# The order of square transfers and the tiles of a weight expansion in a fused attention, MLP and adapter kernel

## The chip, the cores and the metric

The kernel runs on one core of one Trainium2 chip. The core has TensorE (PE; its weight loads are listed as PEld), VectorE (DVE), ScalarE (ACT), GpSimd (POOL) and SyncE (SP). SP, ACT and POOL issue transfers, each on a queue of its own (q1, q10 and q0 in the profile); 16 DMA engines carry them. The metric is the device time of one execution in microseconds. The kernel before took 1170.44 us (median of 3 runs, 1168.72 to 1171.33).

## What is computed

Four sequences of 512 tokens by 512 features, float32. For each sequence b:

```
q, k, v  = x @ Wq, x @ Wk, x @ Wv
attn_out = softmax(q k^T / sqrt(512)) @ v @ Wp + bp
cms      = gelu(attn_out @ cW1 + cb1) @ cW2 + cb2 + one_hot(code_b)     # 512 -> 2048 -> 512
modifier = gelu([attn_out, cms] @ mW1 + mb1) @ mW2 + mb2                # 1024 -> 2048 -> 512
y        = clip(x + cms + modifier, 0, 1)
h        = y + gelu(y @ W_down[s] + b_down[s]) @ W_up[s] + b_up[s]      # s = stream_b, one of 3 adapters
out      = layernorm(h) * ln_w[s] + ln_b[s]
```

## The kernel before

**Products by seven.** Large products are done by a two-by-two block scheme with seven products in place of eight (Strassen's, in Winograd's form), mostly at two levels. Each product needs sums of weight blocks and sums of input blocks. PE does the products, DVE and ACT put them together, and the sums of weight blocks are formed once: `weight_sums` (L236, operations at L238, L241, L242, L243) makes the four sums of a block on POOL. This is called expansion here. Expanded weights go to DRAM (`c1_inner`, `c1_outer`, `c2_kept`, `m1_kept`, `m2_kept`, in the profile `c_inner`, `c_outer`, `c_kept`, `m_kept`) and SP fetches them when the layers run.

**The stages.** The sequences are taken in two pairs. First Wq is folded with Wk, and Wv with Wp (`folded`). Then attention for pair 0 and pair 1 (to about 237 us), then for pair 0 the first cms layer (`c1_layer`, to about 330 us), the second (`second_layer` with cW2, from about 330 us), the two modifier layers, and the same for pair 1 with the adapters of pair 0 between. The expansion of cW1, cW2 and mW1 (`expansion`, L449) runs on POOL beside the attention and the first cms layer, handed out in steps by `steps(expanding, n)`; that of mW2 comes later.

**The tiles.** SBUF is full, so tiles have many uses. `wide` holds slots 0 and 1; slots 2 to 7 are tiles of their own (all shown as `slot` in the profile), 1 MB each; `part` has 1 MB, `first` 0.5 MB. The expansion reads raw weights in slots 4 and 5 and writes slot 1, slot 3, `part` and `first`. Slot 6 holds Wv and slot 7 Wp until they are folded; then they take x of sequences 3 and 2.

**Squares.** `load_squares` (L153) loads x of a sequence of the second pair as 32-by-32 squares, four transfers per sequence, for DVE to transpose (L534). The 128-byte rows make 2048 packets per transfer. The call is at L995, first for sequence 2 (slot 7), then for sequence 3 (slot 6), on SP's queue.

**Order.** A scheduler arranges each engine's instructions from the program's order and its own estimates; what is passed to `tc.keep_in_program_order` keeps its place. Each engine then runs its list in order, and waits by semaphores for what its operands need: a write into a tile waits for transfers that still read it.

**One unit of the expansion.** `expand_c1` (L268) makes one of two units of cW1: sums of one block in the upper half of slot 1 (transfer L275), sums of the outer level into the lower half of slot 1, `part` and `first` (transfers L286 and L287), and the sums of those in slot 1 (transfer L291). Both units use slot 1. `expand` (L378) makes one unit of cW2 or mW1, of which there are two and four, with three tiles that are called one, two and three, here `part`, slot 3 and slot 1:

```
tt(s1, a21, a22, ALU.add)             # lower half of one        (L390)
tt(s2, s1, a11, ALU.subtract)         # lower half of two
tt(s3, a11, a21, ALU.subtract)        # lower half of three
yield from plain((2, a12, one), (1, a11, three), (4, a22, two))   # upper halves, each kept (L393)
tt(block(last), a12, s2, ALU.subtract)                            # into first
then()                                                            # raw weights of the next unit (L376)
yield from full((5, one), (7, three), (6, two))                   # upper halves, whole tile kept
yield from fourth(block(last), one)                               # upper half of one, L407 and L408
```

So tile one is written and kept last, by L408, and the sums for L408 wait until the whole of tile one has been kept for product 5.

**Where the tiles are next used.** In the second cms layer `wide` takes differences of the first layer's outputs: `differences(1, LOW)` writes slot 0 and `differences(1, HIGH)` slot 1 (both L1383, DVE). Behind it on DVE come the sums for the next inner operands (L248) and the additions that empty PE's banks (L1067). `part` takes products of the second layer from the fourth outer product on.

Of the kernel before, what the change touches and what calls it, by code (L numbers as in the profile page):

```python
# [18 lines left out]
def kernel(  # L19
# [38 lines left out]
    nc = tc.nc  # L58
# [36 lines left out]
    slot = [wide[:, 4 * i : 4 * i + 4, :].rearrange("p c n -> p (c n)") for i in range(2)]  # L95
    slot += [const.tile([P, 2048], F32, name=f"slot{i}") for i in range(2, 8)]
    wslot = [const.tile([P, 2048], F32, name=f"wslot{i}") for i in range(4)]
    part = const.tile([P, 4, 512], F32, name="part")
    first = const.tile([P, 2, 512], F32, name="first")
# [41 lines left out]
    def flat(t):  # L141
        return t.rearrange("p c n -> p (c n)")
# [10 lines left out]
    def load_squares(src, dst, eng):  # L153

        squares = src.rearrange("(t r) (d a c) -> a r d t c", r=32, a=4, c=32)
        for a in range(4):
            eng.dma_start(
                out=dst[32 * a : 32 * a + 32].rearrange("p (d t c) -> p d t c", d=4, c=32),
                in_=squares[a],
            )  # L160
        return dst.rearrange("p (d t c) -> p d t c", d=4, c=32)

    def load_blocks(src, dst, eng):
# [10 lines left out]
    def load_c1(u, eng):  # L174
        for m in range(2):
            raw = slot[4 + m].rearrange("p (c h n) -> p c h n", c=4, h=2)
            for h in range(2):
                at = h * HH + m * 512 + u * 256
                eng.dma_start(
                    out=raw[:, :, h, :],  # L180
                    in_=cW1[:, at : at + 256].rearrange("(c p) n -> p c n", p=P),
                )

    wp = rows_of(slot[7])
    for a in range(4):
        nc.sync.dma_start(
            out=wp[32 * a : 32 * a + 32],
            in_=Wp[P * a : P * a + P].rearrange("(c p) n -> p c n", p=32),
# [10 lines left out]
    for v, n in zip(bias_src, counts):  # L199
        nc.gpsimd.dma_start(  # L200
            out=bias_rows[at : at + n, :], in_=v.rearrange("(c p) -> c p", p=P)
# [34 lines left out]
    def weight_sums(a11, a12, a21, a22, s1, s2, s3, s4, eng=None, pinned=False):  # L236
        op = (eng or nc.gpsimd).tensor_tensor
        i = op(s1, a21, a22, ALU.add)  # L238
        if pinned:
            tc.keep_in_program_order(i)  # L240
        op(s2, s1, a11, ALU.subtract)  # L241
        op(s3, a11, a21, ALU.subtract)  # L242
        return op(s4, a12, s2, ALU.subtract)  # L243

    def token_sums(b11, b12, b21, b22, t1, t2, t3, t4, eng=None, pinned=False):
# [16 lines left out]
    c1_inner = {  # L262
        (p, u): spill.tile([P, n], F32, name=f"c1_inner_{p}_{u}")
        for p, n in ((1, 1024), (5, 2048), (2, 1024))
        for u in range(2)
    }

    def expand_c1(u, then):  # L268
        raw = [t.rearrange("p (c h n) -> p c h n", c=4, h=2) for t in slot[4:6]]
        to = slot[1][:, 1024:].rearrange("p (k n) -> p k n", k=4)  # L270
        inner_sums = [to[:, k] for k in range(4)]
        weight_sums(
            raw[0][:, 0, 0, :], raw[0][:, 1, 0, :], raw[1][:, 0, 0, :], raw[1][:, 1, 0, :], *inner_sums
        )
        nc.gpsimd.dma_start(out=c1_inner[1, u], in_=slot[1][:, 1024:])  # L275
        yield
        spaces = (slot[1][:, :1024], flat(part)[:, :1024], flat(part)[:, 1024:], flat(first))
        sums = [t.rearrange("p (m c n) -> p m c n", m=2, c=2) for t in spaces]
        for m in range(2):
            weight_sums(  # L280
                raw[m][:, 0:2, 0, :], raw[m][:, 2:4, 0, :], raw[m][:, 0:2, 1, :], raw[m][:, 2:4, 1, :],
                *(t[:, m] for t in sums),
            )
        then()
        outer = c1_outer[u].rearrange("p k m c n -> p (k m c n)")
        nc.gpsimd.dma_start(out=outer[:, :2048], in_=flat(part))  # L286
        nc.gpsimd.dma_start(out=outer[:, 2048:], in_=flat(first))  # L287
        yield
        s1 = sums[0]
        weight_sums(s1[:, 0, 0, :], s1[:, 0, 1, :], s1[:, 1, 0, :], s1[:, 1, 1, :], *inner_sums)  # L290
        nc.gpsimd.dma_start(out=c1_inner[5, u], in_=slot[1])  # L291
        yield

    def c1_plain(p, g, m):
# [69 lines left out]
    def load_raw(src, is_first, u, raw):  # L364
        for h in range(2):
            dst = raw[h].rearrange("p (c n) -> p c n", c=4)
            for i in range(2):
                if is_first:
                    at = i * HH + u * 256
                    rows = src[h * V : (h + 1) * V, at : at + 256]  # L370
                    to = dst[:, :, i * 256 : (i + 1) * 256]
                else:
                    at = h * HH + i * HH // 2 + u * 256
                    rows = src[at : at + 256, :]
                    to = dst[:, 2 * i : 2 * i + 2, :]
                nc.gpsimd.dma_start(out=to, in_=rows.rearrange("(c p) n -> p c n", p=P))  # L376
# [56 lines left out]
    def expand_all(units, raw, pairs, last, end=None):  # L433
        if last is None:
            load_raw(*units[0][:2], units[0][3], raw)
        for n, unit in enumerate(units):

            def then():
                if n + 1 < len(units):
                    load_raw(*units[n + 1][:2], units[n + 1][3], raw)  # L440
                elif end is not None:
                    end()

            yield from expand(unit, raw, pairs, last, then)

    m1_units = [(mW1, True, m1_kept, u) for u in range(4)]
    m2_units = [(mW2, False, m2_kept, u) for u in range(2)]

    def expansion():  # L449

        c2_units = [(cW2, False, c2_kept, u) for u in range(2)]
        yield from expand_c1(0, lambda: load_c1(1, nc.gpsimd))
        yield from expand_c1(1, lambda: load_raw(cW2, False, 0, slot[4:6]))

        constants()
        yield from expand_all(
            c2_units + m1_units, slot[4:6], (flat(part), slot[3], slot[1]), flat(first)
        )

    def late_expansion():  # L460
# [39 lines left out]
    def steps(gen, n):  # L500
        with tc.issue_after(behind.pop().ins) if behind else nullcontext():
            for _ in range(n):
                next(gen, None)

    expanding = expansion()


# [59 lines left out]
    def constants():  # L567

        nc.gpsimd.tensor_copy(pos, pos_i)


        nc.gpsimd.tensor_copy(code, code_i)
        for b in range(B):
            nc.gpsimd.tensor_scalar(target[:, b, :], pos, code[:, b : b + 1], None, ALU.is_equal)
            nc.gpsimd.tensor_add(target[:, b, :], target[:, b, :], cb2_c)


        nc.gpsimd.tensor_copy(ex, str_i)
        nc.gpsimd.tensor_scalar(wrap, ex, 0.0, float(E), ALU.is_lt, ALU.mult)
        nc.gpsimd.tensor_add(ex, ex, wrap)  # L580
        nc.gpsimd.tensor_scalar(ex, ex, 0.0, float(E - 1), ALU.max, ALU.min)
        nc.gpsimd.tensor_copy(idx_e, ex)
        nc.gpsimd.tensor_scalar(ex_v, ex, float(V), None, ALU.mult)
        nc.gpsimd.tensor_scalar(ex_bn, ex, float(BN), None, ALU.mult)
        for b in range(B):
            nc.gpsimd.tensor_scalar(idx_d[:, b, :], pos, ex_v[:, b : b + 1], None, ALU.add)
            nc.gpsimd.tensor_scalar(idx_u[:, b, :], pos[:, :NB], ex_bn[:, b : b + 1], None, ALU.add)
# [379 lines left out]
    for pair in range(B // 2):  # L967
# [3 lines left out]
        u = big[4 - 2 * pair : 6 - 2 * pair]  # L971
# [18 lines left out]
        if pair == 0:  # L990

            lhs_vp = folded(
                left_operand(wv_t, s_v), rhs_wp, w_vp, s_v, order=(1, 5, 6, 2, 7, 3, 4)
            )
            x_blocks = [load_squares(x[b], flat(x_places[b]), nc.sync) for b in range(2, B)]  # L995
# [719 lines left out]
    for pair in range(B // 2):  # L1715
# [43 lines left out]
        for _ in between:  # L1759
# [4 lines left out]
        spaces = [  # L1764
            (h[3][:, 2 * s : 2 * s + 2], h[1][:, 4 * s : 4 * s + 4], (h[2][:, :4], h[3][:, 4:])[s])
            for s in range(2)
        ]
# [92 lines left out]
```

## Time and profile before

| | |
|---|---|
| median of 3 runs | 1170.44 us |
| the profiled execution's own time | 1169.09 us |
| its span, first to last instruction | 1167.2 us |
| mean granted clock of PE | 0.997 |
| DVE, ACT, POOL busy | 77%, 25%, 51% of the span |
| moved by DMA | 258.88 MB, mean 222 GB/s |
| packets under 512 bytes | 24532 of 101442 |

A line of a timeline has the start in the span, the length (of a merged run of like instructions), engine, line, operation, what is written and read, the shape, a count, and in brackets the idle time of the engine before it and what ended that. Buffer numbers are left out, so all tiles of one name look alike. A line of the table by stretches has the stretch, its length, the busy time of PE, PEld, DVE, ACT and POOL with the number of instructions, the granted clock, the DMA engines' busy share and GB/s. A line on a queue has packets, MB and the share of the 16 engines' time; one on an issue has what is written and read, the queue, the count, the size and the time to landing. A mean over the span says little here, since the stages have different limits: what counts is where PE idles and who ended that wait.

### The profile page before, as it was taken

How to read it: one execution, taken by the hardware profiler on the slowest of the kernel's cores; microseconds unless marked ns; L12 is line 12 of the kernel's file. 1: busy time of each engine (PE TensorE's matmuls, PEld its weight loads, DVE VectorE, ACT ScalarE, POOL GpSimd, SP SyncE). 2: the span in 40 equal slices, each digit the busy share in tenths (PEclk: the TensorE clock that was granted, in tenths of full speed). 3: DMA queues.
4: the chain of work that ended last, by engine and by line, in shares of the span. 5: the costliest groups of instructions: out<-in, count | busy, mean ns of one | idle time of the engine just before them, and what ended most of it. 6: DMA issues, size and time to landing. Idle time of an engine off the chain costs nothing.

```text
span 1167.2 us, 13674 instructions
## 1 busy us (share of the span) xinstructions
PE 1155.0 (99%) x4941; PEld 923.9 (79%) x4941; DVE 894.2 (77%) x1227; ACT 293.9 (25%) x535; POOL 593.0 (51%) x646
## 2 busy tenths in 40 slices
PE   9999999999989999999999999999999999999997
PEld 8588468566458888888888887778888888888875
DVE  5755855487699967898699956689994588689955
ACT  4234326245520000013310037272000003230014
POOL 5789989789970058895200676971000001265401
PEclk9999999999999999999999999999999999999999
DMA  9892973898875488888847562145745464575701
GB/s 293 240 252 97 350 311 132 343 367 285 305 266 210 164 277 325 283 317 323 259 153 288 180 218 90 64 152 184 286 143 189 155 230 167 180 271 198 249 4 72
DMA packets 101442, 258.88 MB, mean 222 GB/s; under 512 B 24532, under 2 KB 59648, under 8 KB 86144
## 3 DMA queue, kind: packets, MB, share of 16 engines
q1 hardware_dynamic: 78144, 159.27, 38.9%
q0 software_dynamic: 20848, 89.18, 21.6%
q10 hardware_dynamic: 2384, 9.57, 2.0%
q8 instruction: 39, 0.64, 0.2%
q14 instruction: 27, 0.22, 0.1%
HBM read 188.78 MB, written 66.06 MB: 218 GB/s over the span
## 4 chain that ended last, share of the span: by engine, by line
PE 72%; POOL 16%; DMA 7%; issue 3%; DVE 1%; DVEq 0%; POOLq 0%
PE i L1363 29%; PE i L1463 28%; PE sum L1205 7%; DMA m_kept<-part 4%; PE down_ps L1570 2%; PE up_ps L1589 2%; POOL part L241 1%; POOL slot L376 1%; POOL part L238 1%; DMA c_outer<-part 1%; POOL part L242 1%; POOL wide L238 1%; PE sum L746 1%; DMA c_kept<-wide 1%; POOL part L243 1%
## 5 line engine op out<-in xcount | busy, mean ns | idle before, releaser
L1363 PE MATMUL i<-slot,wslot 128*128 128x256 f32 x1184 | 261.0, 379 | 0.0
L1363 PEld LDWEIGHTS i<-slot,wslot 128*128 128x128 f32 x1184 | 224.9, 190 | 31.0 <-DMA wslot<-in_L_cond_mW 0.4
L1463 PE MATMUL i<-slot,wslot 128*128 128x256 f32 x896 | 204.6, 381 | 4.5 <-DVE cms L1067 4.1
L1463 PEld LDWEIGHTS i<-slot,wslot 128*128 128x128 f32 x896 | 171.2, 191 | 28.9 <-DVE cms L1067 4.5
L1463 PE MATMUL i<-hidden,wslot 128*128 128x256 f32 x576 | 132.2, 379 | 0.0
L1463 PEld LDWEIGHTS i<-hidden,wslot 128*128 128x128 f32 x576 | 109.4, 190 | 15.7 <-issue 1.0
L1074 ACT COPY first<-i 128x512 f32<-128x512 f32 (+1 forms) x42 | 21.6, 514 | 391.3 <-PE i L1363 234.7
L1067 DVE TENSOR_TENSOR part<-i,part 128x512 f32<-128x512 f32 (+1 forms) x156 | 90.8, 591 | 38.1 <-PE i L1363 27.9
L1096 ACT ACTIVATE hidden<-hidden,bias 128x512 f32<-128x512 f32 x128 | 83.9, 716 | 72.1 <-DVE hidden L590 62.0
L1746 POOL DMA_DIRECT2D slot<-xT_kept x4 | 2.9, 729 | 152.9 <-PE i L1363 152.9
L1205 PE MATMUL sum<-mod,wslot 128*128 128x256 f32 x288 | 66.6, 379 | 0.0
L1205 PEld LDWEIGHTS sum<-mod,wslot 128*128 128x128 f32 x288 | 54.7, 190 | 7.4
L248 DVE TENSOR_TENSOR slot<-hidden 128x1024 f32<-128x1024 f32 x46 | 60.6, 1317 | 0.0
L1749 POOL TENSOR_TENSOR cms<-cms,slot 128x512 f32<-128x512 f32 x16 | 23.9, 1516 | 70.3 <-PE i L1363 38.5
L248 DVE TENSOR_TENSOR slot<-hidden,slot 128x1024 f32<-128x1024 f32 x46 | 56.7, 1232 | 0.3
L1295 PE MATMUL c<-slot,wslot 128*128 128x512 f32 x128 | 55.3, 592 | 0.0
L1067 DVE TENSOR_TENSOR part<-i,first 128x512 f32<-128x512 f32 (+1 forms) x50 | 31.4, 632 | 31.1 <-PE i L1363 20.0
L376 POOL DMA_DIRECT2D slot<-in_L_cond_mW x24 | 17.9, 751 | 72.1 <-DVE slot L248 71.1
L746 PE MATMUL sum<-hidden,wslot 128*128 128x256 f32 x232 | 53.2, 379 | 0.0
L590 DVE TENSOR_TENSOR sum<-sum,wslot 128x512 f32<-128x512 f32 x48 | 33.2, 695 | 24.3 <-PE sum L746 19.6
L590 DVE TENSOR_TENSOR hidden<-part,hidden 128x2048 f32<-128x2048 f32 x20 | 48.9, 2446 | 0.5
L1295 PEld LDWEIGHTS c<-slot,wslot 128*128 128x128 f32 x128 | 24.3, 190 | 30.6 <-issue 28.5
(338 smaller groups left out, 2166.1 us busy)
## 6 DMA issues: line engine op xcount, KB each, us to landing
wslot<-m_kept SPq DMA_DIRECT2D x48, 1024.0 KB, 6.5
wslot<-m_kept SPq DMA_DIRECT2D x36, 512.0 KB, 4.9
wslot<-c_kept SPq DMA_DIRECT2D x16, 1024.0 KB, 6.4
slot<-in_L_cond_mW POOLq DMA_DIRECT2D x24, 512.0 KB, 7.7
wslot<-in_L_cond_mW SPq DMA_DIRECT2D x24, 512.0 KB, 6.3
wslot<-in_L_cond_cW SPq DMA_DIRECT2D x40, 256.0 KB, 5.3
slot<-in_L_cond_cW POOLq DMA_DIRECT2D x12, 512.0 KB, 6.9
m_kept<-wide POOLq DMA_DIRECT2D x6, 1024.0 KB, 8.6
```

The lines of the kernel that those rows point to most:

```text
L238: i = op(s1, a21, a22, ALU.add)
L248: i = eng.tensor_tensor(out_, one, two, ALU.subtract)
L376: nc.gpsimd.dma_start(out=to, in_=rows.rearrange("(c p) n -> p c n", p=P))
L590: nc.vector.tensor_tensor(dst, a, b, ALU.add)
L746: nc.tensor.matmul(v[:, j, :], lhsT=lhs[p][:, c, j * P : (j + 1) * P], rhs=rhs[p][:, c, :], start=(first_ and j == 0 and c == 0), stop=(c ...
L1067: nc.vector.tensor_tensor(dst, ps, other, ALU.add)
L1096: nc.scalar.activation(block[:, t, :], block[:, t, :], AF.Gelu, bias=bias_c[:, 8 * half + t : 8 * half + t + 1],)
L1205: nc.tensor.matmul(halves_of(ps)[:, j, :], lhsT=a[g][:, at_[q], j * P : (j + 1) * P], rhs=rhs[q][:, 0, :], start=(first_ and j == 0), stop ...
L1295: nc.tensor.matmul(ps, lhsT=lhs(c, t), rhs=operands[p][:, c, :], start=(c == 0), stop=(c == 1),)
L1363: nc.tensor.matmul(out_ps[:, j, :], lhsT=a[j][q][:, c, :], rhs=now[q][:, c, :], start=(c == 0), stop=(c == 1),)
L1463: nc.tensor.matmul(ps[:, :256], lhsT=a[k // 2][q][:, k % 2, :], rhs=now[q][:, k, :], start=(k == 0), stop=(k == 3),)
L1749: nc.gpsimd.tensor_tensor(cms[s][:, d, :], cms[s][:, d, :], in_rows[3][:, d, :], ALU.add)
```

## The change

Three edits. The eight square transfers are kept in program order, so they go to SP's queue as four for slot 7 and then four for slot 6; before, the scheduler had put three of slot 6 ahead of those for slot 7. The second unit of cW1 forms its sums in slot 3 instead of slot 1. The units of cW2 and mW1 take slot 1, `part`, slot 3 as one, two and three, instead of `part`, slot 3, slot 1.

```diff
@@ load_squares
         for a in range(4):
-            eng.dma_start(
+            i = eng.dma_start(
                 out=dst[32 * a : 32 * a + 32].rearrange("p (d t c) -> p d t c", d=4, c=32),
                 in_=squares[a],
             )
+            tc.keep_in_program_order(i)
@@ expand_c1
-        to = slot[1][:, 1024:].rearrange("p (k n) -> p k n", k=4)
+        place = slot[(1, 3)[u]]
+        to = place[:, 1024:].rearrange("p (k n) -> p k n", k=4)
...
-        nc.gpsimd.dma_start(out=c1_inner[1, u], in_=slot[1][:, 1024:])
+        nc.gpsimd.dma_start(out=c1_inner[1, u], in_=place[:, 1024:])
         yield
-        spaces = (slot[1][:, :1024], flat(part)[:, :1024], flat(part)[:, 1024:], flat(first))
+        spaces = (place[:, :1024], flat(part)[:, :1024], flat(part)[:, 1024:], flat(first))
...
-        nc.gpsimd.dma_start(out=c1_inner[5, u], in_=slot[1])
+        nc.gpsimd.dma_start(out=c1_inner[5, u], in_=place)
@@ expansion
         yield from expand_all(
-            c2_units + m1_units, slot[4:6], (flat(part), slot[3], slot[1]), flat(first)
+            c2_units + m1_units, slot[4:6], (slot[1], flat(part), slot[3]), flat(first)
         )
```

## The prediction

> **What bounds the kernel now.** I read the page first: the busy line says that TensorE (PE) works for 99% of the span, so what a change in the preparation of weights can give or take is only idle time of PE, or its clock.
>
> ```profile
> PE 1155.0 (99%) x4941; PEld 923.9 (79%) x4941; DVE 894.2 (77%) x1227; ACT 293.9 (25%) x535; POOL 593.0 (51%) x646
> ```
>
> Then the busy times by stretch, to find where PE idles. Outside of the first microsecond and the last 28 us there is one place: 325 to 375 us. The second column is PE's busy time, the value after POOL's count is the granted clock.
>
> ```profile
> 325.00:350.00 25.00, 20.70 (x84) 15.50 (x82) 23.60 (x19) 5.24 (x9) 16.76 (x20) 1.00 0.74 271
> 350.00:375.00 25.00, 24.81 (x107) 21.53 (x108) 24.62 (x32) 0.70 (x2) 0.00 (x0) 0.93 0.45 174
> ```
>
> PE's timeline names the wait, and that of DVE shows what DVE did until it freed PE at 350.19.
>
> ```profile
> 344.17 1.96 PE L1463 MATMUL i<-slot,wslot 128*128 128x256 f32 x8 [0.44 <-ACT mod L1074]
> 350.19 5.41 PE L1463 MATMUL i<-slot,wslot 128*128 128x256 f32 x16 [4.06 <-DVE cms L1067]
> ```
>
> ```profile
> 338.65 4.28 DVE L1383 TENSOR_TENSOR wide<-hidden,hidden 128x2048 f32<-128x2048 f32 x1 [1.36 <-DMA m_kept<-wide]
> 342.86 1.21 DVE L248 TENSOR_TENSOR slot<-hidden 128x1024 f32<-128x1024 f32 x1
> 347.51 2.28 DVE L1383 TENSOR_TENSOR hidden<-hidden,hidden 128x2048 f32<-128x2048 f32 x1
> 349.72 0.75 DVE L1067 TENSOR_TENSOR cms<-i,mod 128x256 f32<-128x256 f32 x2
> ```
>
> The second layer begins at 329.8. DVE must write the upper half of `wide`, which is slot 1, and waits for the last transfer of the expansion that reads slot 1; the four L248, one more L1383 and the sums L1067 that empty PE's banks stand behind it in order. So PE's 4.06 us hang on one thing: when the expansion on POOL gives slot 1 back. POOL's timeline shows the expansion's stalls and its last issue:
>
> ```profile
> 54.48 1.27 POOL L242 TENSOR_TENSOR part<-slot 128x512 f32<-128x512 f32 x1 [7.99 <-issue]
> ...
> 62.20 0.72 POOL L238 TENSOR_TENSOR wide<-slot 128x256 f32<-128x256 f32 x1 [4.04 <-DMA c_inner<-wide]
> ...
> 163.63 0.72 POOL L238 TENSOR_TENSOR part<-first 128x256 f32<-128x256 f32 x1 [2.71 <-DMA c_kept<-part]
> ...
> 334.36 0.55 POOL L393 DMA_DIRECT2D m_kept<-wide  x1
> ...
> 341.27 0.55 POOL L408 DMA_DIRECT2D m_kept<-part  x1
> ```
>
> **The change, step by step.** Compared engine by engine, the two programs have the same instructions in the same order on PE, DVE and ACT; POOL and SP differ.
>
> *1. Squares.* Three of the eight square transfers left SP at 42.07 and landed 13.9 us later; now all eight wait for slot 7, so they start at 59.64, where the fourth does now. On SP nothing is queued behind them before the x rows at 128.85, and the first reader is DVE's L534 at 124.15, over 50 us after they can land: no cost there, and if that cover were gone it would be PE's wait for the second pair. POOL's queue gains in 42 to 56 us and loses later. The five that now run at 59.6 to 70.5 moved 10320 packets in 76.4% of 10.9 us, 1.65 us a square, so three are 5.0 us of all 16 DMA engines that move behind 59.64.
>
> *2. Sums in slot 3.* The 7.99 us stall before 54.48 is the first unit's transfer out of `part` (issued 43.27, 11.1 us to landing: 54.4). POOL now has other work first: a slot-3 sum that needs the third raw load, issued 41.79, landing 7.5 us later at 49.3. The stall becomes 49.3 - 46.5 = 2.8 us, 5.2 saved; `part` is written 5.8 us of work after that, at 55.1, when it is free. The 4.04 us wait for slot 1 is gone. Next is the 0.56 us wait for `part` at 86.74, which slot 1 as first tile avoids. A new wait is possible where POOL overwrites `wslot` at 80.70 now; 9.2 us sooner is 71.5, and PE reads it until 71.5: nothing. Slot 3 now has to drain before its L390: issue to landing was 10.1 us for the same megabyte (80.12 to 90.2), so 70.9 + 10.1 = 81.0 against 80.6 wanted: 0.4 lost. Lead of POOL at 90 us: 5.2 + 4.0 + 0.6 - 0.4 = 9.4; if the three squares hold up everything behind 59.64 by their 5.0 us, 4.4.
>
> *3. What is left of the lead.* Here I choose by this row of transfers, 132 to 164 us:
>
> ```profile
> q0 software_dynamic: 1290, 5.73, 45.5%
> q10 hardware_dynamic: 576, 4.19, 31.1%
> q1 hardware_dynamic: 1018, 2.02, 21.6%
> ```
>
> The 16 DMA engines are busy 98% of 32 us: 31.5 us of work, over half of it x rows and kept results that SP and ACT issue when DVE and PE let them, from 128.85 on, and these don't move. POOL's wait at 163.63 is for a transfer in this jam. Issued earlier it only stands longer in the same queue. Of the work, some 1.0 MB of q0 (its 5.73 less the 4.72 up to and with that transfer, 2.6 us) need not come first. Data starts 1.7 us after an issue (a 1 MB transfer alone took 4.2 us, 2.5 of it at 421 GB/s), so the jam starts at 130.5 and that transfer lands between 130.5 + 31.5 - 2.6 = 159.4 and 162.0, against 163.6: a lead of 1.5 to 4.2 us survives, and the rest comes back as a wait of up to 9 us. I take 2.8, the middle. Behind it POOL waits 3.40, 1.41 and 1.38 us at 213 to 227, 1.13 and 1.99 at 254 to 258, 2.59 at 297, all for its own transfers; a lead can shrink to nothing in these or win some 2 us. I leave it at 2.8.
>
> *4. Tiles in another order.* Now the price. The wait at 338.65 was for the transfer of 334.36, slot 1 being the third tile. As first tile, slot 1 is read by the very last transfer (issue 341.27 now, out of `part`). That one took
>
> ```profile
> m_kept<-part POOLq DMA_DIRECT2D x1, 512.0 KB, 9.8
> ```
>
> because SP's loads, issued at 341.17, ran beside it; the same three transfers ended at 127.20 with
>
> ```profile
> c_kept<-part POOLq DMA_DIRECT2D x1, 512.0 KB, 4.6
> ```
>
> Issued 2.8 us sooner, at 338.5, it is ahead of SP's data (341.17 + 1.7 = 342.9), so I take 4.6: landing 343.1. POOL is then done, and DVE's L1383 takes the 2.28 us of the row at 347.51 in place of 4.28: it ends at 345.4 in place of 342.9. DVE is 2.5 us late, PE idles 6.6 us in place of 4.06.
>
> *Sum.* 0 for PE until 346, + 2.5 us there: 1169.09 + 2.5 = 1171.6 us for the profiled execution, which stands 1.35 under the median of the runs; the median becomes 1170.44 + 2.5 = **1172.9 us**. Equal time needs the transfer to land by 340.65, the last issue by 336.05, a lead of 5.2.
>
> The clock: after the 4.06 us idle the profile grants 0.50 at 352 to 354 us, about 3.4 us in all at half speed, 1.7 us lost, and none after the 0.44 us idle. I leave the 1.7 us as it is. The Trainium skill (TensorE: Matmul & The Clock Gate, "What's actually happening") says that the gate looks at free-running windows of 3413 ns, so a later restart can fall into a second slow window. With a restart at 352.7 that would lose some 0.75 us more, 1173.6; no row here shows a second window.
>
> For the squares, the share of the queues at 46 to 48 us is 45.1% for SP's and 43.6% for POOL's. The Trainium skill (DMA: Bandwidth & Descriptors, "Queues, rings and completion order") says that an engine goes round the queues packet by packet, which by that rule would halve POOL's raw loads behind 59.64 and speaks against the change. It would bring the lead at 90 us to the lower 4.4; by the jam behind 132 us the sum stays the same.
>
> **Rivals.**
> *The lead survives (faster).* The place is the wait at 163.6, and it decides from a lead of 5.2 us on. For it: POOL loses 29 us to stalls between 46 and 309 us, the two longest go, and 88 to 104 us is almost free of transfers. Against it: the jam. With all 9.3 us the last issue is at 332.0, landing 336.6, before DVE is free at 337.3: L1383 ends at 339.6, 3.3 us sooner, PE idles 0.7 us, and the 1.7 us of clock come back: -5.0, 1165.4 us.
> *The lead is lost wholly.* The later stretches set the end and the last issue stays at 341.27, beside SP's loads: landing 351.1, L1383 ends at 353.4, 10.4 us late: 1180.8 us. For it: the waits at 213 to 297 are all for queues that SP shares; against it: POOL starts each of them sooner.
> *Gain and price cancel.* A lead of 4.7 to 5.7 us changes nothing: 1170.4 us.
>
> **How the numbers follow.** Forecast 0.50, with its own range 1171.4 (lead 4.2: landing 341.7, +1.0) to 1175.1 (lead 1.5: landing 344.4, +3.8, and 0.9 for SP's loads beside it); lead survives 0.28; lost 0.14; cancel 0.08. About 0.2%, 2.3 us, is what a measurement of this kernel can tell from no change. Slower by more: 0.37 of the forecast's 0.50 and the 0.14, 0.51. Faster by more: a lead over 6 us, where the clock's 1.7 us come too, 0.20. The rest, 0.29, is within. The range leaves out the far thirds of the two outer rivals: 1166.5 to 1179.5.
>
> **What would show it.** Right: POOL has no stalls of 7.99 and 4.04 us and is about 9 us ahead at 75 us; a wait of 6 to 9 us at about 161 on a transfer out of `wide`; last issue at 337 to 340; DVE's L1383 `wide` waits for that last transfer, 4 us or more, and then takes 2.28; PE's idle before L1463 is 5 to 8 us. Wrong, if POOL passes 164 us over 5 us ahead and DVE finds slot 1 free, or if PE idles anywhere new before 330.

## The result, and the profile after

The changed kernel takes 1175.49 us (median of 22 runs, 1170.23 to 1181.56), the kernel before beside it 1169.72 us (median of 22, 1167.46 to 1172.56). The ratio is 1.0049, 95% interval 1.0033 to 1.0065: slower by 0.5%, or 5.8 us. The 22 times are not one spread. They lie in two groups of eleven, 1170.23 to 1174.33 (median 1171.93) and 1176.65 to 1181.56 (median 1179.67), and the median falls between the two. The gap between them is 2.3 us, the widest between neighbours in the list, with 1.8 us the next. The profiled execution took 1173.6 us (span 1171.7) and is of the lower group; it is read first. The changed file's lines are one or two higher: L1383 is now L1385, L1463 L1465, L1067 L1069, L393 L395, L408 L410, L238 L239.

POOL's timeline of the kernel after (start, length, engine, line, operation, tiles, shape, count, idle before and who ended it), with the waits of the expansion and its last issues:

```profile
46.80 0.73 POOL L239 TENSOR_TENSOR slot<-slot 128x256 f32<-128x256 f32 x1 [1.16 <-DMA slot<-in_L_cond_cW]
...
160.82 0.73 POOL L239 TENSOR_TENSOR wide<-first 128x256 f32<-128x256 f32 x1 [13.03 <-DMA c_kept<-wide]
...
207.37 0.72 POOL L239 TENSOR_TENSOR wide<-first 128x256 f32<-128x256 f32 x1 [0.68 <-DMA m_kept<-wide]
...
254.54 0.72 POOL L239 TENSOR_TENSOR wide<-first 128x256 f32<-128x256 f32 x1 [4.26 <-DMA m_kept<-wide]
295.35 0.73 POOL L239 TENSOR_TENSOR wide<-first 128x256 f32<-128x256 f32 x1 [4.76 <-DMA m_kept<-wide]
...
338.84 0.55 POOL L409 DMA_DIRECT2D m_kept<-first  x1
339.39 0.55 POOL L410 DMA_DIRECT2D m_kept<-wide  x1
```

The stalls of 7.99 and 4.04 us are gone and one of 1.16 is left. Against the same instruction of before, POOL is 11.7 us ahead at 64 us and 13 us ahead as it comes to the wait that ends at 160.82. There it stands 13.03 us where it stood 2.71, and leaves with a lead of 163.63 - 160.82 = 2.8 us. After the wait at 207.37 the lead is 5.5; those at 254.54 and 295.35 take it to 3.9 and 1.7, and the last issue comes 341.27 - 339.39 = 1.9 us sooner.

DVE's timeline after, at the start of the second layer, and that of PE:

```profile
343.50 2.29 DVE L1385 TENSOR_TENSOR wide<-hidden,hidden 128x2048 f32<-128x2048 f32 x1 [8.08 <-issue]
345.71 1.22 DVE L249 TENSOR_TENSOR slot<-hidden 128x1024 f32<-128x1024 f32 x1
...
350.38 2.29 DVE L1385 TENSOR_TENSOR hidden<-hidden,hidden 128x2048 f32<-128x2048 f32 x1
352.58 0.75 DVE L1069 TENSOR_TENSOR cms<-i,mod 128x256 f32<-128x256 f32 x2
```

```profile
347.03 1.97 PE L1465 MATMUL i<-slot,wslot 128*128 128x256 f32 x8 [2.40 <-issue]
353.05 5.41 PE L1465 MATMUL i<-slot,wslot 128*128 128x256 f32 x16 [4.06 <-DVE cms L1069]
```

The last transfer landed at 343.22. DVE's L1385 for `wide` starts 0.28 us later (the profile names no releaser, so it says "issue") and takes 2.29 us in place of 4.28, with POOL done. It ends 2.9 us later than before, and PE idles 2.40 + 4.06 = 6.46 us in place of 4.49. The tables by stretch say the same, 21.59 and 21.95 us of PE's 25 where it had 20.70 and 24.81; the clock falls to half once, for 3.41 us, as before.

```profile
325.00:350.00 25.00, 21.59 (x86) 15.88 (x84) 16.89 (x14) 4.59 (x9) 14.88 (x18) 1.00 0.77 289
350.00:375.00 25.00, 21.95 (x94) 19.01 (x95) 24.66 (x28) 0.37 (x1) 0.00 (x0) 0.93 0.34 127
```

This execution is 4.5 us longer than the profiled one of before. 2.0 us are here. 1.2 are two waits for Wq and Wk at 6 to 8 us, ahead of all that the change touches, and 1.5 a wait for DVE at 503 us in the modifier layer. A second profile of the same kernel (below) has neither 503 us' wait nor those of Wq and Wk in that size, so I count only the 2.0 as the change's in this group. What makes the upper group is the question of the experiments.

### The profile page after: what moved, and what is told of

Its sections match the earlier page's. It is cut to its first block, busy times and chain, and to the rows that moved or that the text cites. A ratio compares the mean times of both kernels' runs of the same rounds, so it can differ in the third digit from the quotient of the medians.

```text
span 1171.7 us, 13665 instructions
## 1 busy us (share of the span) xinstructions
PE 1154.8 (99%) x4941; PEld 923.3 (79%) x4941; DVE 891.7 (76%) x1227; ACT 293.2 (25%) x535; POOL 588.3 (50%) x646
## 4 chain that ended last, share of the span: by engine, by line
PE 68%; DVE 3%; issue 1%; DVEq 0%
PE i L1465 28%; PE i L1365 27%; PE sum L1207 7%; PE down_ps L1572 2%; PE up_ps L1591 2%; DVE slot L249 1%; DVE hidden L592 1%; PE up_ps L1586 1%; DVE part L1069 0%; DVE wide L1385 0%; DVE hidden L1385 0%; DVE hidden L1656 0%; DVE hidden L1666 0%; DVE stats L1681 0%; DVE hidden L1695 0%
## 5 line engine op out<-in xcount | busy, mean ns | idle before, releaser
L1465 PE MATMUL i<-slot,wslot 128*128 128x256 f32 x896 | 204.6, 381 | 6.5 <-DVE cms L1069 4.1
L1465 PEld LDWEIGHTS i<-slot,wslot 128*128 128x128 f32 x896 | 171.2, 191 | 30.8 <-DVE cms L1069 4.5
L1465 PE MATMUL i<-hidden,wslot 128*128 128x256 f32 x576 | 132.2, 379 | 0.0
L1465 PEld LDWEIGHTS i<-hidden,wslot 128*128 128x128 f32 x576 | 109.4, 190 | 15.7 <-issue 1.0
L1069 DVE TENSOR_TENSOR part<-i,part 128x512 f32<-128x512 f32 (+1 forms) x156 | 90.8, 592 | 35.4 <-PE i L1365 25.1
L1751 POOL TENSOR_TENSOR cms<-cms,slot 128x512 f32<-128x512 f32 x16 | 26.8, 1697 | 69.0 <-PE i L1365 38.5
L249 DVE TENSOR_TENSOR slot<-hidden 128x1024 f32<-128x1024 f32 x46 | 60.6, 1318 | 0.0
L249 DVE TENSOR_TENSOR slot<-hidden,slot 128x1024 f32<-128x1024 f32 x46 | 56.7, 1233 | 0.3
L592 DVE TENSOR_TENSOR hidden<-part,hidden 128x2048 f32<-128x2048 f32 x20 | 53.8, 2692 | 0.5
L1069 DVE TENSOR_TENSOR part<-i,first 128x512 f32<-128x512 f32 (+1 forms) x50 | 31.5, 632 | 28.6 <-PE i L1365 17.5
```

Source lines behind the costliest of these rows:

```text
L249: i = eng.tensor_tensor(out_, one, two, ALU.subtract)
L592: nc.vector.tensor_tensor(dst, a, b, ALU.add)
L1069: nc.vector.tensor_tensor(dst, ps, other, ALU.add)
L1465: nc.tensor.matmul(ps[:, :256], lhsT=a[k // 2][q][:, k % 2, :], rhs=now[q][:, k, :], start=(k == 0), stop=(k == 3),)
L1751: nc.gpsimd.tensor_tensor(cms[s][:, d, :], cms[s][:, d, :], in_rows[3][:, d, :], ALU.add)
```

## The experiments

They were run in three sets, each on a chip of its own with the kernel before beside it. Differences are read inside a set. Line numbers of L239 and so on differ by one or two between the kernels.

**The parts one by one.** The first set takes the three edits apart. The squares alone:

```
             i = eng.dma_start(...)        # load_squares, as changed
+            tc.keep_in_program_order(i)
```

> The square transfers alone keep their order; slots and tile order are those of before. If the loss comes by way of slot 1 (my theory), nothing of it is here: without squares beside it the first unit's transfer out of part lands about 3 us sooner (51.4 as in the changed kernel, 54.4 before), so POOL's stall before L242 is about 5 us instead of 7.99, the jam of 132 to 164 us takes most of that, DVE still waits about 1 us for slot 1 as third tile: 1169.7 us, between -1 and +1. If the later squares hold up transfers that matter (rival), the time is 2 to 6 us longer and a wait on a raw load shows at 60 to 90 us.

1170.51 us against 1170.29 of before, ratio 1.0000 [0.9987, 1.0013]. POOL's timeline of this kernel still has its stalls:

```profile
52.99 1.26 POOL L243 TENSOR_TENSOR part<-slot 128x512 f32<-128x512 f32 x1 [6.05 <-issue]
60.33 0.72 POOL L239 TENSOR_TENSOR wide<-slot 128x256 f32<-128x256 f32 x1 [3.68 <-DMA c_inner<-wide]
...
163.64 0.72 POOL L239 TENSOR_TENSOR part<-first 128x256 f32<-128x256 f32 x1 [3.90 <-DMA c_kept<-part]
```

The first shrinks by 1.9 us, and the jam before 163.64 takes it back: 163.64 here, 163.63 before. The order of the squares is worth nothing by itself at the median.

The squares and slot 3 with the old tiles:

```
-            c2_units + m1_units, slot[4:6], (slot[1], flat(part), slot[3]), flat(first)
+            c2_units + m1_units, slot[4:6], (flat(part), slot[3], slot[1]), flat(first)
```

> Squares in order and the second unit's sums in slot 3, but the tiles of later units in the old order (part, slot 3, slot 1). My theory: POOL is about 9 us ahead at 75 us, 2.8 us after the wait at 161, and slot 1, the third tile again, is given back by the transfer of about 331.6, landing at 335.8, before DVE asks at 337.3. DVE does not wait, PE idles 1 to 3 us in place of 4.06: 2 to 4 us faster than before, 1166 to 1168 us. If the loss of the changed kernel sits behind 360 us, in the modifier layers (rival), this kernel is as slow as the changed one, 1173 to 1176 us.

1168.89 us (1163.7 to 1172.06), ratio 0.9981 [0.9964, 0.9998]: a gain of 1.4 us at the median, where 2 to 4 were expected. Its times also come in two groups, five at 1163.7 to 1165.25 and seven at 1168.81 to 1172.06. The profile is of the lower:

```profile
336.60 4.28 DVE L1385 TENSOR_TENSOR wide<-hidden,hidden 128x2048 f32<-128x2048 f32 x1 [1.36 <-DMA m_kept<-wide]
```

DVE starts the difference 2.05 us sooner than before, PE idles 3.00 us and its clock doesn't fall. So a lead of about 2 us is worth something here, and the new order of tiles turns this gain into a loss.

The order of tiles alone, on the kernel before:

```
-            c2_units + m1_units, slot[4:6], (flat(part), slot[3], slot[1]), flat(first)
+            c2_units + m1_units, slot[4:6], (slot[1], flat(part), slot[3]), flat(first)
```

> The tile order alone: no lead, all of the price. My theory: POOL's last transfer reads slot 1 and is issued at about 341, beside SP's two loads, landing at about 350; DVE's L1383 ends 10 us later than before, PE idles about 14 us: 8 to 11 us slower, 1178 to 1181 us. If what counts is the lead alone or something behind 360 us (rival), it is within 3 us of before.

1181.9 us (1181.36 to 1184.78), ratio 1.0107 [1.0091, 1.0123], 11.6 us slower. Lines of POOL, DVE and PE:

```profile
343.06 0.55 POOL L408 DMA_DIRECT2D m_kept<-wide  x1
...
353.41 2.29 DVE L1383 TENSOR_TENSOR wide<-hidden,hidden 128x2048 f32<-128x2048 f32 x1 [19.54 <-issue]
...
356.94 3.75 PE L1463 MATMUL i<-slot,wslot 128*128 128x256 f32 x8 [13.16 <-issue]
```

With no lead, the last issue falls behind SP's loads of about 341 us and lands at 353. PE idles 15.4 us here, and the clock stays at half for 17.07 us, of which PE works for 6.7. With a clock at half, this loses half of the time that PE works: 3.4 us, where before it was 1.7. So 10.94 us of idle and 1.65 of clock are added, 12.6 in all, against 11.6 measured. That is the full price of giving slot 1 back last, and it looks like the upper group, only worse.

**The last unit alone put back.** The changed kernel, but the very last unit takes the tiles in the old order:

```
     def expand_all(units, raw, pairs, last, end=None, final_pairs=None):
...
+            tiles = final_pairs if final_pairs and n + 1 == len(units) else pairs
-            yield from expand(unit, raw, pairs, last, then)
+            yield from expand(unit, raw, tiles, last, then)
...
+            final_pairs=(flat(part), slot[3], slot[1])
```

> The changed kernel, but the very last unit of the expansion takes the tiles in the old order (part, slot 3, slot 1), so that slot 1 is given back by the third-last tile transfer and not by the last. All else in front is the changed kernel's. My theory: DVE finds slot 1 free at 337, PE idles 1 to 3 us, 2 to 4 us faster than before: 1166 to 1168 us. Rival (loss behind 360 us or by the squares): as the changed kernel, 1173 to 1176 us.

1171.16 us (1164.41 to 1173.29), ratio 0.9996 [0.9977, 1.0015]. The price is gone, from 5.8 us to 0.9, but at the median the gain that I expected isn't there: five of the twelve times are at 1164.41 to 1167.8, where I expected them or lower, and seven at 1170.86 to 1173.29. Its profile (1171.67) has the place: the lead is 2.5 us at 161 us and gone at 213.40 (before: 212.91), behind a wait of 6.39 us for the first mW1 unit's keep of tile one. That transfer is issued at 201.69, 0.5 us behind SP's first load for the layer (201.17), and lands at 213.33. In the profile of the changed kernel it is issued at 201.36, 0.56 us ahead of SP (201.92), and lands at 207.30:

```profile
201.36 0.57 POOL L395 DMA_DIRECT2D m_kept<-wide  x1
...
201.92 0.35 SPq L1128 DMA_DIRECT2D slot<-attn_kept  x1
```

Hence a theory for the two groups, A: at 201 us POOL's keep of 1 MB and SP's 2 MB of loads, which start when PE comes to the layer, reach the queues within a microsecond of each other, and whichever is second waits. A lead of 2.8 us puts POOL at the edge of that.

**A second profile of the changed kernel.**

> The changed kernel once more, for a second profile. The 22 times of it so far lie in two groups of 11, 1170.2 to 1174.3 and 1176.7 to 1181.6 us, and the one profiled execution (1173.6) is of the lower. Theory A: a race at 201 us between POOL's 1 MB keep of the first mW1 unit (issued 201.36 in that profile, landed 207.30) and SP's loads for the first layer (issued 201.92): where SP is first the keep lands at 211 to 214 as it does in the profile before, POOL's lead of 2.8 us falls to about nothing, the last transfer of the expansion is issued at 341 to 342 and lands at about 350, and the time is 1176 to 1181. Theory B: the two groups come from the restart of PE near 350 us alone (another count of half clock windows, 1.7 us each) with the lead as it was: landing 343, time up to 1176. If this execution is of the lower group, its keep lands by 208 and its last transfer by 344.

1170.34 us, one execution, level with the kernel before beside it (1170.40) and again of the lower group: keep issued 200.60, SP 201.09, landed 208.76. The last issue is at 337.83, landed 341.66, and PE idles 1.67 + 4.05 us. The keep landed somewhat later than the 208 that I gave this group; the rest is as expected, and no test of the theory yet.

**SP's loads taken away.**

```
-    load_attn(0, (6, 7))
```

> The changed kernel without SP's two 1 MB loads of the first layer's attention weights at 201 and 213 us (left out: the layer multiplies by what is in the two slots). POOL, PE, DVE and ACT keep their order. Theory A (the race at 201 us): the keep has nothing to race with but two 512 KB loads, lands by 208 in every execution, the lead of 2.8 us survives or grows to 4 or 5, the last transfer is issued at 336 to 339 and lands at 341 to 343.5; no execution over 1175, median 1169 to 1172. Theory B (the clock alone): still two groups, with a median of about 1175.

1168.91 us (1164.07 to 1172.75, 12 runs) against 1170.40, ratio 0.9980 [0.9964, 0.9997]. The keep, issued at 202.05, landed at 208.50, a little later than forecast, and no execution came near 1176. For A, but the changed kernel was timed only once in this set, so the chip was not ruled out. That is why it is repeated below.

**Less in the jam at 132 to 164 us.**

```
-            nc.scalar.dma_start(out=xT_kept[2 * pair + k], in_=xT[k])
+            if pair == 0:
+                nc.scalar.dma_start(out=xT_kept[k], in_=xT[k])
...
-  ... in_=xT_kept[2 * pair + s]
+  ... in_=xT_kept[s]
```

> The changed kernel without the four 512 KB stores of the transposed x of the second pair (left out: that pair later reads the first pair's). These 2 MB, some 5 us of all 16 DMA engines at the 421 GB/s of a lone transfer, leave the jam of transfers at 132 to 164 us. Step 3 of the prediction (the jam takes most of the lead): the wait of 13.0 us at 160.8 shrinks to about 8, POOL is 6.5 to 8 us ahead of before behind it in place of 2.8, its keep at about 197 lands before SP's loads of 201, the last transfer of the expansion lands at or before 340, DVE's L1385 for `wide` waits at most 2 us, PE idles at most 2.5 us near 350; median 1165 to 1168 in one group. Rival: the waits at 213, 254 and 297 us set the end whatever the lead is: median 1170 to 1176.

1167.02 us (1164.0 to 1170.23, 8 runs), ratio 0.9976 [0.9960, 0.9992]. The wait is shorter, as the jam would have it:

```profile
158.19 0.73 POOL L239 TENSOR_TENSOR wide<-first 128x256 f32<-128x256 f32 x1 [8.62 <-DMA c_kept<-wide]
...
337.04 0.53 POOL L410 DMA_DIRECT2D m_kept<-wide  x1
```

The lead behind it is 5.4 us in place of 2.8 (6.5 to 8 expected), the keep goes out at 198.74, 2.4 us ahead of SP, and there is no upper group. But I had the last transfer landing by 340 and PE idle for at most 2.5 us; it landed at 340.85 and PE idled 4.90, because waits of 0.8 to 5.2 us between 211 and 293 take the lead back to 4.2. So the jam takes most of the early gain, as forecast, and the later waits take a further part of whatever passes it.

**The keep made later, and SP's loads taken away, on one chip.** The third set has the changed kernel, two that are to move the race either way, and a candidate. Every kernel of this set is some 15 us longer than elsewhere, the one before too (1185.15; one of its 19 times is 1171.15). All four profiles show a wait of PE of 10.9 to 12.4 us between 681 and 707 us, and 13.65 us of half clock from there, in no profile of the other chips, and far from what is compared. So absolute times forecast for this set are off by it, and I go by differences.

> The changed kernel, timed beside the next three on one chip, since its two groups of times (1170.2 to 1174.3 and 1176.7 to 1181.6 us) may be a matter of the chip. Theory A (race at 201 us between POOL's keep and SP's loads): two groups again, with a share of 2 to 8 in 10 above 1175.5, whatever the chip. If the profiled execution is over 1175.5, its keep of 201 us lands at 210 to 214 and its last transfer at 346 to 351; if under, by 209 and by 344. Rival (the chip, or the clock): one group here.

Median 1192.18 us, ratio 1.0050 [1.0026, 1.0075], the same ratio as at first. Two groups again: four at 1184.18 to 1187.66 (median 1187.2, 2.1 over before) and six at 1191.76 to 1196.46 (median 1193.9, 8.7 over). The profile, 1191.76 us, is one of the upper group, the lowest of it. SP's and then POOL's timeline of it:

```profile
201.15 0.35 SPq L1128 DMA_DIRECT2D slot<-attn_kept  x1
```

```profile
201.58 0.57 POOL L395 DMA_DIRECT2D m_kept<-wide  x1
...
211.46 0.72 POOL L239 TENSOR_TENSOR wide<-first 128x256 f32<-128x256 f32 x1 [4.54 <-DMA m_kept<-wide]
...
339.57 0.56 POOL L409 DMA_DIRECT2D m_kept<-first  x1
340.12 0.55 POOL L410 DMA_DIRECT2D m_kept<-wide  x1
```

SP is 0.43 us ahead this time. The keep lands at 211.39, the lead drops from 2.7 to 1.5 us where in the first profile it had risen to 5.5, and the last issue is at 340.12, 1.2 us ahead of SP's loads for the second layer (341.30). DVE and PE:

```profile
347.85 2.29 DVE L1385 TENSOR_TENSOR wide<-hidden,hidden 128x2048 f32<-128x2048 f32 x1 [11.71 <-issue]
```

```profile
351.37 3.50 PE L1465 MATMUL i<-slot,wslot 128*128 128x256 f32 x8 [7.52 <-issue]
357.39 5.41 PE L1465 MATMUL i<-slot,wslot 128*128 128x256 f32 x16 [2.52 <-DVE cms L1069]
```

An issue only 0.7 us later than in the first profile cost DVE 4.35 us. SP's loads also came 0.8 us sooner (342.07 in the first profile), so the last transfer is 1.2 us ahead of them where it was 2.7; it now runs beside them and lands at 347.57, 7.45 us after its issue, where it took 3.8. PE idles 10.04 us here, 5.5 more than in the profile before. The half clock around 350 us lasts 10.24 us in place of 3.41, but PE idles in part of it and works in 6.5 us of it, so 1.6 us more are lost. Together 7.1 us; this execution stands 6.6 over the median of before, and the group 8.7.

The keep made later: one of the sums ahead of it is done twice more, 1.4 us of POOL in all.

```
             for p, t in sums:
                 inner_sums(block(t[:, :1024]), t[:, 1024:])
+                if p == 5 and src is mW1 and u == 0 and last is not None:
+                    s = sums_of(t[:, 1024:])
+                    for _ in range(2):
+                        tt(s[:, 3], block(t[:, :1024])[:, 2:4, :P], s[:, 1], ALU.subtract)
                 keep(p, t)
```

> The changed kernel with two POOL sums of 0.7 us done three times over ahead of the one keep at 201.36 us, which is so issued 1.4 us later, at 202.8, behind SP's loads of 201.9; nothing else. Theory A: the keep always loses the race, lands at 210 to 214 as it does in the profile before (212.84); POOL has no lead left, the last transfer is issued at 341 to 342 and lands at 346 to 351, PE idles 9 to 14 us near 350, and 8 in 10 or more of the executions are over 1175.5, median 1176 to 1181. Rival (there is no such race, and a delay costs what it is): the wait of 0.7 us behind it shrinks to nothing, 0.7 us of lead are lost, median 0.7 above that of the changed kernel beside it, with the same share over 1175.5.

1196.51 us (1196.17 to 1196.76), ratio 1.0095 [1.0080, 1.0111]. There is no lower group. SP and POOL:

```profile
201.54 0.35 SPq L1132 DMA_DIRECT2D slot<-attn_kept  x1
```

```profile
204.92 0.57 POOL L395 DMA_DIRECT2D m_kept<-wide  x1
205.49 0.55 POOL L395 DMA_DIRECT2D m_kept<-slot  x1
214.26 0.72 POOL L239 TENSOR_TENSOR wide<-first 128x256 f32<-128x256 f32 x1 [6.11 <-DMA m_kept<-wide]
```

The keep lands at 214.19 and the last issue is at 342.60. The delay came out larger than meant, since the scheduler also put the next product's sums ahead of the keep (the two keeps now go out together): the POOL work added is 1.4 us, but the keep goes out 3.3 us later than in the profile above. The time is 2.6 us over the upper group's median and 9.3 over the lower's. The rival had 0.7 us over the changed kernel with both groups, for a delay of 1.4 us, and this didn't come. But a plain delay of 3.3 us, without any race, would take the last issue from the 339.39 of the first profile to 342.7, and it is at 342.60. So this run doesn't tell the race from a mere delay.

SP's loads taken away again, beside it:

> The changed kernel without SP's two loads of the first layer's attention weights (left out: the layer multiplies by what is in the two slots), again, now beside the changed kernel itself. On the chip of its first run none of 12 executions was over 1172.8, median 1168.9. Theory A: the same here, at most 1 in 10 over 1175.5, median 1168 to 1171, while the changed kernel beside it has two groups. Rival (the chip): both kernels in one group, the same median within 2 us.

1181.92 us (1179.57 to 1185.67, 9 runs), ratio 0.9968 [0.9952, 0.9983]. All nine lie under 1187.7, where the changed kernel has six of ten over 1191, and its profile has no wait at 207 to 214 at all. With the keep later, all are of the upper group; with SP's loads gone, none; as it is, half.

What this shows is the far end: the price is paid where the last transfer meets SP's loads for the second layer. Over the kernels in which slot 1 is given back last, that half megabyte landed 3.8 us after an issue at least 2.7 us ahead of those loads, 7.45 us after one 1.2 us ahead, and 10.0 to 10.1 us after one behind them. The chip alone as cause falls, since both groups come back on the third chip. That the order of the two issues at 201 us picks the group is argued, not shown. For it are three profiles of the unedited kernel, one of them of the upper group, and that no time is in the upper group without SP's loads. But those 2 MB are also 2 MB less to move, the keep made later is also a delay, and the leads of 5.5, 4.1 and 1.5 us behind the wait at 207 to 211 us are 1.9, 3.4 and 1.2 at the last issue: the waits in between undo most of what the race does. The kernel with the old tiles doesn't fit it: its profile lost the race (SP 0.39 us ahead, landed 211.59) and is of its lower group, so what splits its times stays open.

**A version that gives slot 1 back sooner.** Squares and slot 3 as changed, the old tiles, and in the last unit product 7, which is made in slot 1, ahead of product 5:

```
...
-            yield from full((5, one), (7, three), (6, two))
+            if final:
+                yield from full((7, three), (5, one), (6, two))
+            else:
+                yield from full((5, one), (7, three), (6, two))
...
```

> The squares and the sums in slot 3 as changed, the tiles in the old order, and the last unit of the expansion with product 7 (out of slot 1) ahead of product 5 (out of `part`), so that slot 1 is given back one product sooner. The kernel with the old order of tiles measured 1168.9, half of its executions near 1164 and half near 1169.5; there slot 1's last transfer was the one before last. Theory (the end hangs on the transfer out of slot 1): it is issued some 5 us sooner, lands at 331 to 335 even where the lead at 201 us is lost, DVE never waits for it, PE idles under 1 us near 350, so all executions are at 1164 to 1166. Rival: PE's idle of 3.0 us in that kernel has another cause (DVE's own work at 337 to 347, that takes 4.28 us for L1385 beside POOL): median 1168 to 1170 as without it.

1164.46 us (1163.07 to 1167.92, 8 runs) against 1170.40: ratio 0.9958 [0.9942, 0.9975], 6 us faster than before. The last transfer out of slot 1 is issued at 326.38, and DVE and PE don't wait:

```profile
326.38 0.57 POOL L395 DMA_DIRECT2D m_kept<-wide  x1
```

```profile
332.77 3.50 DVE L1388 TENSOR_TENSOR wide<-hidden,hidden 128x2048 f32<-128x2048 f32 x1
```

```profile
325.00:350.00 25.00, 25.00 (x106) 19.68 (x105) 24.72 (x23) 3.68 (x7) 17.18 (x16) 1.00 0.75 280
350.00:375.00 25.00, 25.00 (x117) 22.00 (x116) 24.66 (x29) 0.74 (x2) 0.00 (x0) 1.00 0.69 271
```

Fifty of fifty microseconds, at full clock. On the third chip:

> Squares and sums in slot 3 as changed, the old order of tiles, and product 7 ahead of product 5 in the expansion's last unit. It measured 1164.46 us against 1170.4 of before on the chip of its first run, ratio 0.9958 [0.9942, 0.9975]. Theory (its end hangs on the transfer out of slot 1, which is now 5 us sooner, so a lost lead at 201 us does not reach PE): again 1163 to 1168, ratio 0.994 to 0.997, no execution over 1170. Rival (the gain was the chip's, or luck of the race): 1166 to 1170.

1181.28 us (1178.6 to 1183.88, 7 runs) against 1185.15, ratio 0.9975 [0.9939, 1.0012]. Lower by 3.9 us, but this interval takes in no change: the first set carries the gain, the second agrees in sign and doesn't confirm its size. There DVE wrote `wide` at 336.53 without a wait, 3.8 us later than in the profile above, behind its own work beside POOL, and PE idled 2.54 us. So with slot 1 free, DVE's own work still sets an idle time near the 3.00 us that the kernel with product 5 first had: the cause that the rival of the first of these two runs names is still at work. DVE's earlier difference for `wide` took 2.81 us in the first of the two profiles, 5.08 in the second and 4.23 with product 5 first, the longer the later POOL's sum into `first` ended (316.47, 319.61 and 318.25 us). So part of the gain can come from where POOL happens to stand beside DVE. And the ratio with this edit, 0.9958 [0.9942, 0.9975], and that without it, 0.9981 [0.9964, 0.9998], have intervals that overlap.

## Why the prediction was right or wrong, point by point

The forecast was 1172.9 us, range 1166.5 to 1179.5; measured 1175.49. The direction and the mechanism hold. The forecast's case is what half of the executions do, and the rival that was given 0.14 is nearly what the other half does. That the median lies within the range is in part luck: it falls in the gap between the groups, and the upper group's own median is above the range.

- *Step 1, squares.* Right: nothing by themselves, ratio 1.0000. Of the two figures for the lead at 90 us, 9.4 and 4.4, the upper was nearer and still low.
- *Step 2, sums in slot 3.* Right in kind, low in size: the lead is 12 to 13 us where 9.4 was summed. The first stall shrank by 6.8 us, not by 5.2 (the third raw load landed at 46.74, not 49.3). POOL entered this stretch 0.85 us ahead already. No wait came at slot 3's L392, since its transfer took 8.65 us and not 10.1. The page's rule in the prediction, from the Trainium skill (DMA: Bandwidth & Descriptors, "Queues, rings and completion order"), was taken to halve POOL's raw loads behind 59.64. This profile shows no such loss: the four raw loads issued at 59.92 to 63.37 landed after 4.3 to 7.3 us, the same four before after 4.0 to 9.1, and POOL waits for none of them.
- *Step 3, first half.* Right: the jam gave back all but 1.5 to 4.2 us, taken as 2.8, measured as 2.8, 3.6 and 2.7 in three profiles of the changed kernel. The extra lead of step 2 went into the wait, 13.03 us in place of "up to 9". The 1.7 us from issue to data was rough: of the 1 MB issued at 334.36 before, packets ran from 1.1 to 3.8 us after the issue, some 390 GB/s.
- *Step 3, second half.* This is the step that fell short: "a lead can shrink to nothing in these or win some 2 us. I leave it at 2.8." I took a middle where there are two outcomes. At 201 us the lead grows (2.8 to 5.5, in the second profile 3.6 to 4.1) or falls (2.7 to 1.5), as the keep goes out ahead of SP's loads or behind them, and at the last issue 1.9, 3.4 and 1.2 us of it are left. With 1.2, the last transfer meets SP's loads and PE pays 7.1 us; with 1.9 it pays 2.0. The trace before had both issues, the keep at 204.19 and SP at 201.04: a lead of 2.8 to 3.6 puts them within a microsecond of each other. That could have been read.
- *Step 4, tiles in another order.* Right for the lower group: landing 343.22 (343.1 forecast), L1385 at 2.29 us (2.28), its end at 345.8 (345.4), PE's idle 6.46 us (6.6), one clock dip of 3.41 us. Two terms cancelled: the issue was 0.9 us later than taken, the transfer 3.8 us and not 4.6. The lower group's median is 2.2 us over before, forecast 2.5. For a lead of 1.5 I gave 344.4, with "0.9 for SP's loads beside it"; at a lead of 1.2 the transfer took 7.45 us where 4.6 was taken and landed at 347.57, so this term is 2.9 us and not 0.9.
- *The clock.* "I leave the 1.7 us as it is" holds in the lower group's profiles. In the upper group's, 3.3 us are lost, 1.6 beyond that. The Trainium skill (TensorE: Matmul & The Clock Gate, "What's actually happening") has windows of 3413 ns: the half-clock stretches of the profiles near 350 us are 3.41, 6.83 and 17.07 us, that is one, two and five times that, and in the upper group's 6.83 and then 3.41. Where they begin in PE's idle time, only the part in which PE works is lost. The second window that no row of before showed is shown here. It came with 5.4 us of idle (the squares alone) and with 4.9 (the jam eased), and not with 6.46, so the idle time doesn't decide the number of windows by itself.
- *The rivals.* "The lead is lost wholly" had 1180.8 us; the upper group's median is 1179.7, with a lead of 1.2 left in its profile. That the numbers agree so well is in part luck, since it had the transfer landing at 351.1, and it landed at 347.57. Its chance, 0.14, was too low by far. "The lead survives" was not seen: none of the first 22 times is under 1170.23.

So the sum is 0.5 x 2.2 + 0.5 x 10.0 = 6.1 us at the mean of the two groups, against 5.8 at the median and 2.5 forecast.

## What to carry to other kernels

A lead won early is worth only what is left where the result is consumed: follow it through every queue on the way, and expect a busy queue to give back nearly all of it. Where a lead brings two transfers on different queues to within a microsecond or two of each other, forecast two outcomes with a price each, not a middle one; a time whose executions split into groups can be a sign of it. And when tiles are permuted, look at which one is given back last in the very last round and who needs it first: with the squares and slot 3 as changed and that product put earlier (product 7 ahead of product 5), the kernel was 6 us faster than before in one set, where the change as made was 5.8 us slower; a second set had 3.9 us, not clear of no change.

## What the runs showed of the hardware that was not expected

- How long a transfer takes depends on its place against another queue's. POOL's megabyte at 201 us landed after 5.9 and 8.2 us when it was issued 0.56 and 0.49 us ahead of SP's 2 MB, and after 9.8 us when it was 0.43 us behind. The last half megabyte landed after 3.8 us when it was issued 2.7 us ahead of SP's next 2 MB, after 7.45 us when 1.2 us ahead, and after 10.1 us when 1.8 us behind.
- POOL and DVE slow each other. In the profile after, at 330.83 us, a POOL sum takes 1.70 us beside DVE's L249 (1.74 us), and one of the same shape 0.73 at 335.55, when DVE is idle, while L249 takes 1.22 with POOL idle (at 345.71, above):

```profile
330.21 1.74 DVE L249 TENSOR_TENSOR slot<-hidden 128x1024 f32<-128x1024 f32 x1
...
330.83 1.70 POOL L239 TENSOR_TENSOR part<-part 128x256 f32<-128x256 f32 x1
...
335.55 0.73 POOL L239 TENSOR_TENSOR wide<-first 128x256 f32<-128x256 f32 x1
```

- Idle time of PE costs more than itself, but not by half of the time at half clock. Near 350 us, 15.4 us of idle with the order of tiles alone came with 17.07 us at half clock, and PE worked for 6.7 of these: 3.4 us of work lost on top. The idle 3.00 us with the old tiles came with none, and 2.54 us on the third chip (product 7 first) with 3.41 us at half clock.
